# A graph network layer on one core: edge lists laid out ahead on the host, and the list test moved behind the first products

## The chip, the cores and the metric

The kernel runs on one core of one Trainium2 chip. The metric is the device time of one launch in microseconds; lower is better. The program's own names are used throughout: PE is the matrix engine, DVE the vector engine, ACT the scalar (activation) engine, POOL the general one, SP the engine that issues most of the transfers (DMAs). Each engine executes its own instructions in their order and waits where data or buffers are missing.

## What is computed

A graph with 1250 nodes of 1024 features and 41,250 directed edges (source, destination, type 0 or 1), sorted by destination, passes through two layers, each with a residual:

```
h = relu(layernorm(x))
# layer 0: relational convolution
n = ln_weight * h * rsqrt(mean(h*h) + 1e-6)
out = n @ W_root + bias
for r in (0, 1):                       # edge types
    w = (edge_type == r)
    sums = segment_sum(n[src] @ W_rel[r] * w, dst)
    out += sums / max(segment_sum(w, dst), 1)
x = x + h + elu(out) @ wo
# layer 1: attention over the same edges
h = relu(layernorm(x)) @ W
e = exp(-leaky_relu((h @ a_l)[src] + (h @ a_r)[dst], 0.1))
x = x + elu(segment_sum(e * h[dst], src) / (segment_sum(e, src) + 1e-5))
```

W_root and each W_rel[r] are 1024x286, wo is 286x1024, W is 1024x1024.

## The kernel before

Nodes are cut into ten row tiles of 128 (the last has 98). The gather and the sum over edges are done with a count matrix: for each pair of nodes and each edge type, how many edges join them. With it the sums over edges become matrix products, and both layers use it.

**Building the counts.** The sorted edges are cut into 110 groups of 375, and each group into three chunks of 125. For one chunk, DVE compares an index row with one number per edge and so gets a matrix of zeros and ones ("key", L505, 125x320), PE multiplies it with the one-hot matrix of the low seven bits of the source ("lo", L480, one for two groups) and adds up the three chunks of a group in PSUM (L506). ACT then copies the 16 destination columns of that group to their place in the counts (L513); where they start is read from a list at run time (L511). An edge that belongs to the next group's first destination is carried over (L509). All this holds only if a group's destinations lie within 16 nodes and neighbouring groups fit together. Where some group doesn't, a general version of the whole kernel (general_arm) does the work.

**The start (gnn_kernel, L1135 to L1234).** The three edge lists are loaded with 110 groups on the partitions. DVE makes the first and last destination of each group, counts the groups that don't fit (L1188 to L1199), and makes from the lists the numbers that the keys need; PE turns them so that the edges of a chunk lie on the partitions (L1221, L1227). Then every engine loads the count of misfits and branches (L1233, L1234): zero leads to fast_arm, and only there do norms and products begin. The given inputs lead to fast_arm.

**First stage of fast_arm (L469 to L654).** The order on PE, DVE and ACT is the one in which the code is written; no scheduler changes it. For each row tile there are 16 product steps (L648: two halves of the joined weights times eight blocks of 128 features). Between the product steps the code puts chunks of the count (`some`), as many as keep step with the products: five ahead, and the rest spread evenly over 154 of the 160 steps (L650). At fixed steps it also puts the statistics (L528), the norm (L541) and the transposes (L559) of tiles further on, and the three parts in which the last tile's product is scaled and split into three bf16 terms (L583 to L600). The statistics of tile t + 2 stand at steps 6 and 9 of tile t. Five buffers hold keys, so DVE can be at most five keys ahead of PE. POOL adds h to x by a transfer that accumulates (L573).

**Loads.** SP issues x's tile 0, the weights of eight blocks (two transfers for each block, W_rel and W_root, L1151 and L1152), tile 1 after the fourth block, and then the other tiles. A semaphore is used again after eight transfers, so an issue may have to wait until an earlier transfer has landed; the issues behind it wait too.

**After that** come the means (L711) and the way back through wo (L753), the attention layer's products (L787, L858), and its weights and sums (L931 to L998). The change doesn't touch them.

Of the kernel before, what the change touches and what calls it, by code (L numbers as in the profile page):

```python
# [8 lines left out]
F32 = mybir.dt.float32  # L9
# [401 lines left out]
def fast_arm(tc, ctx, w_root, conv_bias, wo, w_gat, a_gat, out,  # L411
             ident, eps5, eps6, lnw, const, wt, wcat, bias, xs, cnt_raw,
             meta, keys, lows, hot_ck, ck, bases, iota_lo, iota_key, iota_ck):
# [56 lines left out]
    with ExitStack() as c1:  # L470
        hot = c1.enter_context(tc.tile_pool(name="hot", bufs=5))
        work = c1.enter_context(tc.tile_pool(name="work1", bufs=2))
# [17 lines left out]
        def chunks():  # L490

            for q in range(NG):
# [10 lines left out]
                for j in range(J):  # L503
# [6 lines left out]
                    if j == J - 1:  # L510
                        b = nc.values_load(bases[0:1, q:q + 1], engines=[mybir.EngineType.Activation],  # L511
                                           min_val=0, max_val=N - 1)
                        nc.scalar.activation(cnt_w[:, :, bass.ds(b, W)], a3, AF.Copy)  # L513
# [21 lines left out]
        def norm(t):  # L535
            n, mv, rstd = ROWS[t], mvs.pop(t), rstds.pop(t)
            nc.vector.reciprocal(rstd[:n], rstd[:n])
            nmr = small("nmr")
            nc.vector.scalar_tensor_tensor(nmr[:n], mv[:n, 0:1], -1.0, rstd[:n], op0=ALU.mult, op1=ALU.mult)
            hs_[t] = h = work.tile([128, D], F32, name="h")  # L540
            nc.scalar.activation(h[:n], xs[t][:n], AF.Relu, bias=nmr[:n], scale=rstd[:n])  # L541
# [19 lines left out]
        def scaled(t, g):  # L561

            n, (hT, pts) = ROWS[t], hTs[t]
            for i in range(4):
                k = 4 * g + i
                if g == 0:
# [34 lines left out]

        for i in range(2):
            statistics(0, i)
        low_hots(0)
        carry_hots(0, 10)
        norm(0)
        some(4)
# [3 lines left out]
        some(1)  # L611
        scaled(0, 1)
        done, ahead = 5, 5
        SK = 2 * KD
        for t in range(T):
            pys[t] = ps.tile([128, 2, 512], F32, name="mm")
            for i in range(SK):
                r, k = divmod(i, KD)
# [9 lines left out]
                if t == 0 and i in (1, 2):  # L628
                    statistics(1, i - 1)
                if t == 0 and i == 3:  # L630
                    norm(1)
                if t == 0 and i in (5, 7):
                    square(i // 6)
# [16 lines left out]
                want = min(NG * J, ahead + -(-(NG * J - ahead) * (t * SK + i + 1) // (T * SK - 6)))  # L650
# [426 lines left out]
def gnn_kernel(  # L1077
# [12 lines left out]
    a_gat: bass.AP,  # L1090
    out: bass.AP,
):
    nc = tc.nc
    D = x.shape[1]
    F = w_root.shape[1]
    HF = F // 2
    KD = D // 128
    assert x.shape[0] == N and NG * GE == src.shape[0] and HF * 2 == F
# [4 lines left out]
    ident = const.tile([128, 128], F32, name="ident")  # L1103
    make_identity(nc, ident)
    ones = const.tile([128, 1], F32, name="ones")
    nc.vector.memset(ones, 1.0)
# [3 lines left out]
    nc.vector.memset(eps6, 1e-6)  # L1110
    lnw = const.tile([128, KD], F32, name="lnw")

    nc.scalar.activation(lnw[:, 0:1], eps5, AF.Sqrt)
    bias = const.tile([128, F], F32, name="bias")

    meta = const.tile([128, 2376], F32, name="meta")
    parts, at = [], 0
    for size in (NG * J, NG * J // 2, NG * T, 3 * 128, T * W, T, NG, NG + 1):
# [6 lines left out]
    iota_key, iota_ck, ck = parts[4].bitcast(F16), parts[5].bitcast(F16), parts[6]  # L1125
    info = parts[7][0:1].bitcast(I32)

    xs = [big.tile([128, D], F32, name=f"x{t}", tag=f"x{t}") for t in range(T)]
    cnt_raw = big.tile([128, 2 * T * NPAD], F16, name="cnt")


    wt = [big.tile([128, D + 2], F32, name=f"w{k}") for k in range(KD)]
    wcat = [w[:, :3 * F].rearrange("p (r f) -> p r f", r=2) for w in wt]

    with ExitStack() as ec:  # L1135
        ep = ec.enter_context(tc.tile_pool(name="ep", bufs=1))
        eps = ec.enter_context(tc.tile_pool(name="eps", bufs=2, space=PSUM))
        eraw = ep.tile([NG, 3, GE], I32, name="eraw")
        for i, (a, eng) in enumerate(((dst, nc.sync), (src, nc.scalar), (etype, nc.gpsimd))):
            eng.dma_start(eraw[:, i, :], a.rearrange("(q e) -> q e", q=NG))  # L1140
        lnw_row = ep.tile([KD, 128], F32, name="lnw_row")
        nc.scalar.dma_start(lnw_row, ln_w.rearrange("(k p) -> k p", p=128))
        nc.scalar.dma_start(bias, _bcast_rows(conv_bias, 128, F))

        def load_x(t):
            nc.sync.dma_start(xs[t][:ROWS[t]], x[t * 128:t * 128 + ROWS[t], :])

        load_x(0)
        for k in range(KD):
            ks = slice(k * 128, (k + 1) * 128)  # L1150
            nc.sync.dma_start(wcat[k][:, :, :F], w_rel[:, ks, :].rearrange("r p f -> p r f"))  # L1151
            nc.sync.dma_start(wcat[k][:, :, F:], w_root[ks, :].rearrange("p (r f) -> p r f", r=2))  # L1152
            if k == 3:
                load_x(1)
        for t in range(2, T):
            load_x(t)

        nc.gpsimd.iota(iota_lo, pattern=[[1, 128], [0, 2 * J]], base=0, channel_multiplier=0,
                       allow_small_or_imprecise_dtypes=True)
        nc.gpsimd.iota(iota_key, pattern=[[1, 2 * T * W]], base=0, channel_multiplier=0,  # L1160
                       allow_small_or_imprecise_dtypes=True)
        nc.gpsimd.iota(iota_ck, pattern=[[1, 2 * T]], base=1, channel_multiplier=0,
                       allow_small_or_imprecise_dtypes=True)
        nc.gpsimd.memset(cnt_raw.rearrange("p (c n) -> p c n", n=NPAD)[:, :, N:], 0.0)


        end = ep.tile([NG, 1], F32, name="end")
        nc.vector.tensor_scalar(end, ident[:NG, NG - 1:NG], N - 4096.0, 4096.0, op0=ALU.mult, op1=ALU.add)

        dstf = ep.tile([NG, GE], F32, name="dstf")  # L1170
        nc.vector.tensor_copy(dstf, eraw[:, 0, :])
        first = ep.tile([NG, 1], F32, name="first")
        nc.vector.tensor_reduce(first, dstf, AX.X, ALU.min)
        below = ep.tile([NG, 1], F32, name="below")
        nc.vector.tensor_scalar_add(below, first, -4096.0)
        pn = eps.tile([128, 1], F32, name="pn", bufs=1)
        nc.tensor.matmul(pn[:NG], ident[:NG, 1:NG + 1], below, start=True, stop=True)
        last = ep.tile([NG, 1], F32, name="last")
        nc.vector.tensor_reduce(last, dstf, AX.X, ALU.max)
        last2 = ep.tile([NG, 1], F32, name="last2")  # L1180
        nc.vector.tensor_reduce(last2, dstf[:, :GE - PE_], AX.X, ALU.max)
        after = ep.tile([NG, 1], F32, name="after")
        nc.vector.tensor_tensor(after, pn[:NG], end, ALU.add)

        step = ep.tile([NG, 1], F32, name="step")
        nc.vector.tensor_tensor(step, after, first, ALU.subtract)
        odd = ep.tile([NG, 1], F32, name="odd")
        nc.vector.tensor_scalar(odd, last, first, float(W), op0=ALU.subtract, op1=ALU.is_ge)  # L1188
        nc.vector.scalar_tensor_tensor(odd, step, float(W), odd, op0=ALU.is_gt, op1=ALU.add)
# [79 lines left out]
```

## Time and profile before

| what | us |
|---|---|
| three timed runs | 636.57, 637.62 (median), 639.51 |
| the profiled execution | 635.77 |
| its span in the profile | 634.0 |
| PE busy in the span | 608.8 (96%) |
| DVE busy | 394.4 (62%) |
| ACT busy | 190.7 (30%) |
| POOL busy | 40.1 (6%) |
| first stage's products (L648), 320 instructions, PE busy | 145.3 |
| counts (L506), 330 instructions, PE busy | 74.4 |
| keys (L505), 330 instructions, DVE busy | 85.4 |

A product step is two PE instructions, since the float32 product takes two passes. In a line of the timeline the first number is the start in the span, the second the time covered; then come the engine, the line of the kernel, the operation, what is written and read, how many instructions are merged into it, and in brackets how long the engine stood idle before it and who released it. Instructions on one engine overlap at their ends, so the mean duration of one is more than the distance from one to the next.

In a line of the windows each engine has its busy time and, in brackets, the number of its instructions, in the order PE, PE's weight loads, DVE, ACT, POOL; then come the clock that PE was granted (1.00 is full), the busy share of the 16 DMA engines, and GB/s.

### The profile page before, as it was taken

Reading aid. Unit: us, or ns where it says so; the run is one execution under the profiler, and the core shown is the slowest. Engines: PE = TensorE matmul, PEld = TensorE weight load, DVE = VectorE, ACT = ScalarE, POOL = GpSimd, SP = SyncE. Lnnn points to the kernel's source line nnn. Section 1 sums busy time; section 2 is a strip of 40 time slices with the busy share of each in tenths; the row PEclk is TensorE's granted clock in tenths of the full one; section 3 lists DMA queues with packets and bytes.
Section 4 is the critical chain, followed back from the end, with each engine's and each line's share of the span. In section 5 each row is a group of like instructions: output and inputs, shape, how many; then the busy total and the mean of one; then the engine's idle time right before and its main releaser. Section 6 shows DMA issues by size and latency. Waiting matters only on the chain.

```text
span 634.0 us, 7896 instructions
## 1 busy us (share of the span) xinstructions
PE 608.8 (96%) x2816; PEld 416.1 (66%) x2816; DVE 394.4 (62%) x969; ACT 190.7 (30%) x354; POOL 40.1 (6%) x52
## 2 busy tenths in 40 slices
PE   2999999999999999999999999999999999999995
PEld 1566666666656756767656888888766666666653
DVE  6788898988772798556676231215445556666642
ACT  2555555555542023320301232222022112222210
POOL 3100000000000000000000000000010111111110
PEclk9999999999999999999999999999999999999999
DMA  7961111011108400000092000000000000000001
GB/s 228 261 198 35 33 35 34 2 34 34 26 1 304 126 1 0 2 1 1 1 169 39 2 1 1 1 0 1 0 1 33 34 33 34 34 34 33 34 35 31
DMA packets 26634, 30.19 MB, mean 48 GB/s; under 512 B 14209, under 2 KB 19068, under 8 KB 26584
## 3 DMA queue, kind: packets, MB, share of 16 engines
q1 hardware_dynamic: 24059, 21.39, 11.3%
q0 software_dynamic: 1488, 5.29, 4.5%
q10 hardware_dynamic: 1037, 2.90, 1.5%
q8 instruction: 24, 0.39, 0.3%
q14 instruction: 26, 0.21, 0.1%
HBM read 16.06 MB, written 5.12 MB: 33 GB/s over the span
## 4 chain that ended last, share of the span: by engine, by line
PE 87%; DVE 5%; DMA 4%; SPq 1%; issue 1%; ACT 0%; ACTq 0%; POOL 0%; DVEq 0%; POOLq 0%
PE mm L648 18%; PE mm L982 16%; PE mm L858 11%; PE p L982 8%; PE acc L506 7%; PE mm L711 7%; PE z L858 4%; PE mm L753 4%; PE mm L787 3%; PE p L994 3%; DMA w<-in_L_gnn_W_rel_dram 2%; DVE scr L699 2%; PE p L787 1%; PE tp L559 1%; DMA rest_w<-in_L_gnn_wo_weight_dram 1%; DMA x<-in_x_dram 1%
## 5 line engine op out<-in xcount | busy, mean ns | idle before, releaser
L648 PE MATMUL mm<-w,hT 128*128 128x429 f32 (+1 forms) x320 | 145.3, 538 | 0.0
L982 PE MATMUL mm<-h,z 128*128 128x342 f32 (+1 forms) x360 | 118.5, 450 | 0.0
L505 DVE TENSOR_SCALAR key<-meta 125x320 bf16<-125x320 f16 x330 | 85.4, 300 | 20.9 <-PE acc L506 10.5
L982 PEld LDWEIGHTS mm<-h,z 128*128 128x128 f32 (+1 forms) x360 | 68.4, 190 | 34.9
L506 PEld LDWEIGHTS <-lo 125*128 125x128 bf16 x330 | 40.8, 126 | 58.0 <-issue 38.3
L506 PE MATMUL acc<-key,lo 125*128 125x320 bf16 x330 | 74.4, 306 | 4.3 <-DVE key L505 4.3
L711 PE MATMUL mm<-y,cnt 128*128 128x286 bf16 (+3 forms) x600 | 75.2, 284 | 3.1 <-DVE x L755 2.9
L513 ACT ACTIVATE cnt<-acc 128x320 f32 x110 | 49.9, 454 | 80.2 <-PE acc L506 72.2
L711 PEld LDWEIGHTS <-cnt 128*128 128x128 f16 (+1 forms) x600 | 59.4, 99 | 17.5 <-issue 4.1
L982 PE MATMUL p<-h,z 128*128 128x341 f32 (+1 forms) x180 | 66.1, 449 | 0.0
L648 PEld LDWEIGHTS mm<-w,hT 128*128 128x128 f32 (+1 forms) x320 | 51.3, 191 | 3.3 <-issue 2.1
L982 PEld LDWEIGHTS p<-h,z 128*128 128x128 f32 (+1 forms) x180 | 33.7, 188 | 17.7
L858 PE MATMUL mm<-w,a 128*128 128x257 f32 (+3 forms) x192 | 44.8, 380 | 0.0
L858 PEld LDWEIGHTS mm<-w,a 128*128 128x128 f32 (+1 forms) x192 | 35.6, 187 | 6.0 <-ACT h L884 0.4
L753 PE MATMUL mm<-wo,meta 128*128 128x512 f32 (+1 forms) x80 | 37.6, 592 | 0.0
L951 POOL TENSOR_TENSOR w<-w,x 128x1024 f32<-128x1024 f32 x9 | 23.4, 2597 | 135.3 <-ACT w L947 120.7
L931 DVE SCALAR_TENSOR_TENSOR z<-z 128x1280 f32<-128x1280 f32 (+2 forms) x11 | 31.2, 2847 | 0.3
L972 DVE TENSOR_SCALAR inv<-mm 128x1 f32<-128x1 f32 x9 | 1.4, 158 | 47.6 <-PE mm L982 47.6
L934 ACT ACTIVATE z<-z 128x1280 f32<-128x1280 f32 (+2 forms) x11 | 12.9, 1173 | 58.8 <-DVE z L933 58.8
L480 DVE TENSOR_TENSOR lo<-meta 125x768 bf16<-125x768 f16 x55 | 30.2, 549 | 0.0
L947 ACT ACTIVATE w<-mm,inv 128x684 f32<-128x684 f32 x9 | 7.5, 832 | 74.2 <-DVE w L946 74.2
L935 DVE TENSOR_TENSOR z<-cnt,z 128x1280 f32<-128x1280 f16 (+2 forms) x11 | 15.1, 1371 | 13.4 <-ACT z L934 13.4
(181 smaller groups left out, 728.9 us busy)
## 6 DMA issues: line engine op xcount, KB each, us to landing
x<-in_x_dram SPq DMA_DIRECT2D x9, 512.0 KB, 5.0
x<-h POOLq DMA_DIRECT2D x9, 512.0 KB, 4.6
out_dram<-w SPq DMA_DIRECT2D x9, 512.0 KB, 3.0
w<-in_L_gnn_W_dram SPq DMA_DIRECT2D x8, 512.0 KB, 4.9
w<-in_L_gnn_W_rel_dram SPq DMA_DIRECT2D x8, 286.0 KB, 6.7
w<-in_L_gnn_W_root_dram SPq DMA_DIRECT2D x8, 143.0 KB, 4.5
wo<-in_L_gnn_wo_weight_dram ACTq DMA_DIRECT2D x2, 512.0 KB, 6.7
a<-in_L_gnn_a_dram ACTq DMA_DIRECT2D x2, 512.0 KB, 5.1
```

The lines of the kernel that those rows point to most:

```text
L480: nc.vector.tensor_tensor(los[q // 2], iota_lo, lows[:, q:q + 2, :].rearrange("p q j -> p (q j)")[:, None, :].to_broadcast([PE_, 128, 2 * J]),
L505: nc.vector.tensor_scalar(key, iota_key, keys[:, q, j:j + 1], None, op0=ALU.is_equal)
L506: nc.tensor.matmul(acc[:, :2 * T * W], los[q // 2][:, :, (q % 2) * J + j], key, start=(j == 0), stop=(j == J - 1))
L513: nc.scalar.activation(cnt_w[:, :, bass.ds(b, W)], a3, AF.Copy)
L648: nc.tensor.matmul(pys[t][:ROWS[t], r, :F + HF], hTs[t][0][:, k, :ROWS[t]], wcat[k][:, r, :], start=(k == 0), stop=(k == KD - 1))
L711: nc.tensor.matmul(pm[:n, r, :f], cnt[:k, h, r, t * 128:t * 128 + n], ybs[h][:k, s, r, :f], start=(h == 0 and s == 0), stop=(h == T - 1 an ...
L753: nc.tensor.matmul(po[:n, c, :], oT[:, i, :n], wo_of[i][:, cs], start=(i == 0), stop=False)
L787: nc.tensor.matmul(o, hT[:, k, :n], wg[k][:, c0:c1], start=(k == 0), stop=(k == KD - 1))
L858: nc.tensor.matmul(o[:a.shape[2], :c1 - c0], a[:, k, :], b[k][:, c0:c1], start=(start and k == 0), stop=(k == KH - 1), skip_group_check=no ...
L931: nc.vector.scalar_tensor_tensor(z, z, 0.1, z, op0=ALU.mult, op1=ALU.min)
L951: nc.gpsimd.tensor_add(high, high, xs[s][:n].rearrange("p (h c) -> p h c", h=2))
L982: nc.tensor.matmul(o, z[:ROWS[t], t, :n], hs[t][:ROWS[t], c0:c1], start=(t == 0), stop=(t == T - 1))
```

## The change

1. **Lists and weights laid out on the host.** Four more inputs are given, all of them rearrangements: the lists by edge within the chunk, group and chunk (`edges`, 125 rows of 990 numbers), every 375th destination (`firsts`), the first weights joined (`w_cat`, so that one transfer of 3432-byte rows loads a block), and ln_weight in columns. The transposes of the lists on PE go, with their copies out of PSUM.
2. **The loads first.** SP's loads of x and the weights are the first instructions of the kernel; lists, firsts and bias are loaded by ACT's queue, all three lists as one transfer.
3. **No branch at the start.** Norm, transposes and first products of tile 0 come ahead of the keys. The numbers for the keys are made on DVE between them. No key is made ahead; the count begins two steps late (`late = 2`). For tile 0 the product steps go block by block over both halves, statistics of tile 1 stand at steps 5 and 6 (1 and 2 before), its norm at step 7 (3 before), and the norm's h is written in two halves.
4. **The test later.** In step 1 of tile 1 DVE measures how far any edge lies outside of what the fast way allows, with a transpose on PE in the middle. In step 6 of tile 1 ACT branches on the result and would clear the counts; the other engines jump there too.
5. **The branch at the end.** fast_arm always runs; if the test found a misfit, general_arm runs after it and writes the output again.

The core of the diff:

```diff
-        for i in range(2):
-            statistics(0, i)
-        low_hots(0)
-        carry_hots(0, 10)
-        norm(0)
-        some(4)
+        room = [yh.tile([128, F + 3 * (F + 2)], F32, name=f"room{t}", tag=f"yh{t}") for t in (9, 8, 7)]
+        raw = room[0][:PE_, :3 * NG * J].bitcast(I32).rearrange("p (i q j) -> p i q j", i=3, j=J)
+        nc.scalar.dma_start(raw, edges)
+        nc.scalar.dma_start(first, _bcast_rows(firsts, PE_, NG))
+        nc.scalar.dma_start(bias, _bcast_rows(conv_bias, 128, F))
...
+        nc.gpsimd.tensor_copy(firstf, first)
+        nc.gpsimd.tensor_tensor(step[:, :NG - 1], firstf[:, 1:], firstf[:, :NG - 1], ALU.subtract)
...
+        nc.vector.tensor_scalar(tile_of, raw[:, 0], 7, None, op0=ALU.logical_shift_right)
+        norm(0)
+        nc.vector.scalar_tensor_tensor(block, tile_of, 2.0, raw[:, 1], op0=ALU.mult, op1=ALU.add)
+        nc.vector.tensor_tensor(d, raw[:, 2], first[:, :, None].to_broadcast([PE_, NG, J]), ALU.subtract)
+        nc.vector.scalar_tensor_tensor(keys, block, float(W), d, op0=ALU.mult, op1=ALU.add)
         for g in range(2):
             turn(0, g)
         scaled(0, 0)
-        some(1)
+        nc.vector.scalar_tensor_tensor(lows, tile_of, -128.0, raw[:, 0], op0=ALU.mult, op1=ALU.add)
         scaled(0, 1)
-        done, ahead = 5, 5
+        low_hots(0)
+        def carried():
+            nc.vector.tensor_tensor(ck, d[:, :, J - 1], step, ALU.is_equal)
+            nc.vector.scalar_tensor_tensor(ck, block[:, :, J - 1], 1.0, ck, op0=ALU.add, op1=ALU.mult)
+            carry_hots(0, 10)
+        def count_over():
+            nc.vector.tensor_tensor(over, d, limit, ALU.subtract)
+            nc.vector.scalar_tensor_tensor(over, d, -1.0, over, op0=ALU.mult, op1=ALU.max)
+            nc.vector.scalar_tensor_tensor(over[:, :, 0], step, -float(W), over[:, :, 0], op0=ALU.add, op1=ALU.max)
+            nc.vector.tensor_tensor(over[:, 0, 0:1], over[:, 0, 0:1], firstf[:, 0:1], ALU.max)
+            worst = small("worst")
+            nc.vector.memset(worst, 0.0)
+            nc.vector.tensor_reduce(worst[:PE_], over, AX.XY, ALU.max)
+            pt = bank("tp")
+            nc.tensor.transpose(pt[:1, 0, :], worst, ident)
+            nc.vector.tensor_reduce(worst[:1], pt[:1, 0, :], AX.X, ALU.max)
+            nc.vector.tensor_scalar_max(n_odd, worst[:1], 0.0)
+        def clear_if_odd():
+            odd = nc.values_load(n_odd, engines=[mybir.EngineType.Activation], min_val=0, max_val=8192)
+            with tc.If(odd > 0):
+                nc.scalar.activation(cnt_raw, eps6.to_broadcast([128, 2 * T * NPAD]), AF.Copy, scale=0.0)
+        done, ahead, late = 0, 0, 2
...
-                r, k = divmod(i, KD)
+                r, k = divmod(i, KD) if t else (i % 2, i // 2)
...
-                if t == 0 and i in (1, 2):
-                    statistics(1, i - 1)
                 if t == 0 and i == 3:
+                    carried()
+                if t == 0 and i in (5, 6):
+                    statistics(1, i - 5)
+                if t == 0 and i == 7:
                     norm(1)
...
+                if t == 1 and i == 1:
+                    count_over()
+                if t == 1 and i == 6:
+                    clear_if_odd()
...
-                want = min(NG * J, ahead + -(-(NG * J - ahead) * (t * SK + i + 1) // (T * SK - 6)))
+                want = min(NG * J, -(-NG * J * max(t * SK + i + 1 - late, 0) // (T * SK - 6 - late)))
...
+    load_x(0)
+    for k in range(KD):
+        nc.sync.dma_start(wt[k][:, :3 * F], w_cat[k * 128:(k + 1) * 128, :])
+        if k == 3:
+            load_x(1)
+    for t in range(2, T):
+        load_x(t)
...
-    n_odd = nc.values_load(info[0:1, NG:NG + 1], min_val=0, max_val=4 * NG + N)
-    with tc.If(n_odd == 0) as which:
-        with ExitStack() as arm:
-            fast_arm(...)
-    with which.Else():
+    with ExitStack() as arm:
+        fast_arm(...)
+    odd = nc.values_load(n_odd, min_val=0, max_val=8192)
+    with tc.If(odd > 0):
         with ExitStack() as arm:
             general_arm(...)
```

## The prediction

> **What bounds the kernel now.** I read the page first. TensorE (PE) is busy 96% of the span and holds 87% of the chain that ended last; of the 40 slices only the first is nearly empty. So time can be won only ahead of the first products and wherever PE waits later in that stage. Next I read the timeline from 0 to 40 us: which instruction opens each step, and what released it.
>
> ```profile
> 12.05 0.14 DVE L1199 TENSOR_TENSOR meta<-po,info_f 1x1 int32<-1x1 f32 x1 [0.68 <-PE po L1195]
> 12.95 1.29 DVE L528 BATCH_NORM_STATS2 st<-x 128x6 f32<-128x512 f32 x2 [0.75 <-DMA w<-in_L_gnn_W_root_dram]
> 15.49 1.24 ACT L541 ACTIVATE h<-x,nmr,rstd 128x1024 f32<-128x1024 f32 x1 [0.68 <-DVE nmr L539]
> 18.87 1.64 PE L648 MATMUL mm<-w,hT 128*128 128x429 f32 x2
> 26.92 0.69 DVE L528 BATCH_NORM_STATS2 st<-x 128x6 f32<-128x512 f32 x1 [1.51 <-DMA x<-in_x_dram]
> 28.70 0.91 PE L648 MATMUL mm<-w,hT 128*128 128x429 f32 x2
> ```
>
> The list test ends at 12.19; 0.76 us later, past the branch, the first statistics start; the first product starts at 18.87. Seen alone, that promises all the time from 5 to 19 us. But the fifth line shows a second gate: VectorE (DVE) waits 1.51 us for the third row tile (x2), and PE then stands until the next keys. The chain of waits over the first 36 us says it more strongly: up to 26.92 it runs through loads, not through the test.
>
> ```profile
> 1.64 6.75 DMA w<-in_L_gnn_W_rel_dram
> 9.21 3.14 DMA w<-in_L_gnn_W_rel_dram
> 12.96 4.43 DMA w<-in_L_gnn_W_rel_dram
> 20.91 5.99 DMA x<-in_x_dram
> 26.92 0.69 DVE st L528
> ```
>
> From 28.35 us PE runs with almost no gap to the stage's end at 197. Hence my yardstick is not the first product but the **eighth** of tile 0 (i = 7), the first one behind the wait for x2: 28.70 before. What is won there, less PE work that is put off and new stalls, is won at the end: the later stages have the same instructions in the same order.
>
> **When x2 lands after the change.** Up to x2 the queues carry the lists (0.495 MB), firsts and bias (0.20), three row tiles (1.57) and eight weight tiles (3.51): 5.78 MB. What the 16 engines can do is in the windows (the last two columns are DMA share and GB/s):
>
> ```profile
> 6.00:8.00 2.00, 0.61 (x3) 0.45 (x3) 2.00 (x8) 0.02 (x1) 0.07 (x1) 1.00 0.89 285
> 8.00:10.00 2.00, 0.72 (x4) 0.63 (x4) 1.79 (x7) 0.50 (x1) 0.00 (x0) 1.00 0.49 166
> 20.00:22.00 2.00, 1.78 (x7) 0.70 (x6) 2.00 (x7) 0.45 (x1) 0.00 (x0) 1.00 1.03 137
> 22.00:24.00 2.00, 2.00 (x10) 1.10 (x8) 1.93 (x8) 0.96 (x3) 0.00 (x0) 1.00 1.07 343
> 28.00:30.00 2.00, 1.65 (x10) 1.22 (x11) 1.97 (x9) 1.77 (x4) 0.00 (x0) 1.00 1.01 236
> ```
>
> The queue was already nearly full (share about 1), apart from holes such as 8 to 10 where SP waits for a semaphore. The change saves holes and small pieces (16 weight transfers become 8 with rows of 3432 bytes), not bytes. I take 343 GB/s: 5.78 MB = 16.9 us. To it come the start of data at 1.8 us (the window 0 to 2 moved only 50 KB), the residual transfer of tile 0, which falls inside this stretch (software queue: 4.5% of 634 us for ten = 2.85 us each), and 1.0 us until a waiter sees the last byte (between 0 and 1.6: DVE saw the destination list at 4.48, while it and the source list, 0.32 MB, need 1.1 us at 285 GB/s from 1.8). x2 lands at **22.5 us** instead of 26.9. Bounds: 419 GB/s, the best window (204 to 206 us), with the residual hidden gives 16.6; 236 GB/s gives 30.1.
>
> [...]
>
> **What stands before that gate.** x0 is now SP's first issue, at 0.74; the row tiles' shortest landing is 4.0 us and the median of the page 5.0, so about 5.3. From statistics to the start of h took 2.54 us (12.95 to 15.49); one list operation (shift, 0.84 on 375 elements; I take 0.5) is put between; half of h is 0.62, four transposes 1.06, one scaling 0.28, hand-overs 0.1: first product at 5.3 + 5.1 = 10.4 us, against 18.87. If the lists land after x0's statistics, that shift holds the reciprocal behind it on DVE, then ACT's h and PE; up to 10 us that costs nothing, since x2 is late anyway. Then PE does seven products (0.72 each in the chain) and nine key matmuls (0.135); DVE makes keys from about 12.5, does the carry flags, the statistics of tile 1 and stands at x2's statistics at about 17.7. So it is the load that ends last, by 4.8 us. The list work moved here (block, difference, keys, lows, carry: seven DVE operations of 0.23 to 0.55, about 3 us) lies in that wait and costs nothing; without it, some 2 us. The POOL operations (firsts, steps, limits) stand ahead of tile 0's residual or in its shadow; nobody waits before the test.
>
> **At the eighth product.** After x2: statistics 0.65, two keys 0.43, hand-over, two key matmuls: x2 + 1.3 = 23.8 us. Before it was 28.70. **Gained 4.9.**
>
> **What is given back.**
> 1. Norm of tile 1 now comes after x2's first statistics: its h (1.24) delays the first transposes, 1.98 us from the eighth to the ninth product against 1.52 before, of which half is made up by the key matmuls: **0.25**.
> 2. Keys put off: by the seventh product 18 were done before (5 ahead and 13), now 9 (two slots late). Nine times 0.135: **1.2** of PE time later. Nothing hides it, PE being the bound.
> 3. The test, now in tile 1 on a DVE that is busy 15.4 us in 18. Two operations of 330 elements (0.81 and 0.76 on 572: 0.47 + 0.44), one of 110 (0.33), single elements and a clear (0.23), a reduction (0.52) = 2.0; PE's transpose 0.34; reduction and clamp 0.41; the next key 0.25: **3.0** between one key and the next. PE holds the transpose in order, with product, keys and everything else behind it. Cover: five key tiles, about 2.4 slots of 1.05 us. DVE's own waits show how much it stays ahead:
>
> ```profile
> 38.09 0.52 DVE L505 TENSOR_SCALAR key<-meta 125x320 bf16<-125x320 f16 x2 [0.53 <-PE acc L506]
> 40.19 0.52 DVE L505 TENSOR_SCALAR key<-meta 125x320 bf16<-125x320 f16 x2 [0.48 <-PE acc L509]
> 43.59 0.30 DVE L505 TENSOR_SCALAR key<-meta 125x320 bf16<-125x320 f16 x1 [0.51 <-PE acc L506]
> 53.98 0.52 DVE L505 TENSOR_SCALAR key<-meta 125x320 bf16<-125x320 f16 x2 [0.42 <-PE acc L506]
> ```
>
> Where DVE waits for PE its lead is full. From 43.59 to 53.98 it never waits: that lead is used up. So only the waits between test and that stretch (0.48 + 0.51) absorb anything: 3.0 - 1.0 = **2.0**. Bounds 0.5 (the five tiles cover it) and 3.3 (nothing does).
> 4. Branches: every engine jumps once in tile 1, ACT also loads the register. The old test and branch took 0.76 us in all, and ACT is idle almost half this stage: **0.2**, bounds 0 and 0.8. The last branch lies beside the last store (issued until 629.20, span end 634.0): nothing; uncovered, 0.76.
>
> **Sum:** 4.9 - 0.25 - 1.2 - 2.0 - 0.2 = 1.25, say **1.3 us faster**. The profiled execution took 635.77 (span 634.0 and 1.77 around it) and would become 634.5; the three timed runs have a median of 637.62, and carried there it is **636.3 us**.
>
> **Rivals.**
> *The load comes early* (36%). At 370 GB/s, between 343 and the best window, and with the residual half hidden, x2 lands at 15.6 + 1.4 + 2.8 = 20; the key lead covers half the test. Eighth product at 21.3: 7.4 - 0.25 - 1.2 - 1.0 - 0.1 = 4.9 faster, 632.7. For it: large rows, fewer issues, and holes like 8 to 10 us that go. Against: 236 GB/s with row tiles alone at 28 to 30, at full share.
> *The load comes late, slower* (16%). In the new instruction order SP's fourth weight load waits for the lists' semaphore, then x1's load for x0's and the next ones for the first weights'; if the lists are late, the queue behind them runs dry and x2 lands at 26 (a mean of 285 GB/s, as at 6 to 8 us). Eighth product at 27.3: 1.4 - 0.25 - 1.2 - 3.3 - 0.5 = 3.9 slower, 641.5. With my test cost it decides from x2 landing at 23.75 on. For it: the holes of before are waits of the same kind; against: eight transfers may be outstanding.
> *The work is not really ahead* (within the forecast): the first product may start at 10.4 or 14 without changing the end, so an early first product alone proves no gain.
>
> **Chances.** The forecast has 48% (634.4 to 640.8), the early load 36%, the late one 16%. A measurement of this kernel tells about 0.5% (3.2 us) from no change, so faster 0.36, same 0.48, slower 0.16. Range 631.5 to 640.8: from the early case with the best cover and a run's scatter of 1 us to the edge of the late case.
>
> **What would show it.** Right: first product near 10 to 12 us, DVE waiting some 3 to 5 us for x2 at its statistics, PE idle beside it, eighth product near 23.8; a PE gap of up to 2 us at the transpose of the test, small gaps until the end of tile 1; from the means on, everything shifted by one amount. Wrong: no wait for x2 (the DMA term falls), a wait for the lists above 10 us, a gap at the branches over 1 us, or a longer tail behind the last store.

## The result, and the profile after

| | before | after |
|---|---|---|
| median of ten runs (lowest to highest), us | 637.47 (636.22 to 639.51) | 641.13 (640.48 to 643.32) |
| profiled execution; its span | 635.77; 634.0 | 640.75; 638.9 |
| x2 at its statistics | 26.92 | 25.73 |
| eighth product of tile 0 | 28.70 | 27.20 |
| end of the first stage (third part of the last tile) | 200.04 | 202.45 |
| split of wo's last rows (high_w) | 211.15 | 215.68 |
| last DVE operation | 627.74 | 632.24 |

After over before is 1.0061, 95% interval 1.0046 to 1.0076: **slower by 0.6%**, 3.7 us, where 1.3 us faster was forecast. The pair of profiles differs by more (5.0 us), since before's profiled execution is faster than any of its timed runs in the table; a second pair of profiles, below, differs by 5.3.

The timeline of after, in the same columns as in the prediction:

```profile
7.45 1.29 DVE L535 BATCH_NORM_STATS2 st<-x 128x6 f32<-128x512 f32 x2 [6.49 <-DMA x<-in_x_dram]
11.54 0.33 DVE L627 TENSOR_SCALAR room<-room 125x330 int32<-125x330 int32 x1 [2.55 <-DMA room<-in_edges_dram]
15.21 4.44 PE L706 MATMUL mm<-w,hT 128*128 128x429 f32 x6
25.73 0.69 DVE L535 BATCH_NORM_STATS2 st<-x 128x6 f32<-128x512 f32 x1 [3.05 <-DMA x<-in_x_dram]
26.68 0.42 PE L513 MATMUL acc<-key,lo 125*128 125x320 bf16 x1 [2.75 <-DVE key L512]
27.20 1.64 PE L706 MATMUL mm<-w,hT 128*128 128x429 f32 x2
40.97 0.27 PE L654 MATMUL tp<-ident,worst 128*1 128x128 f32 x1 [0.85 <-DVE worst L652]
```

The form is the forecast one: an early first product (15.21, before 18.87), then DVE standing for x2 and PE for the keys behind it. But the lists land only at 11.54 and x2 at 25.73, and the eighth product takes 1.64 us (0.91 before). The chain of waits now runs to x2 through the small `firsts`, which lie behind the lists:

```profile
1.39 12.44 DMA meta<-in_firsts_dram
13.85 0.33 SPq L1177
14.18 0.04 issue
14.22 0.48 SPq L1177
14.70 0.04 issue
14.75 10.96 DMA x<-in_x_dram
25.73 0.69 DVE st L535
```

Among the waits of SP's queue in the first 30 us, one stands out (total, times, longest):

```profile
SPq L1177 <- DMA room<-in_edges_dram: 8.7, 1, 8.7
```

And the windows (columns as before):

```profile
6.00:8.00 2.00, 0.00 (x0) 0.00 (x0) 0.55 (x1) 0.00 (x0) 0.00 (x0) 1.00 1.04 295
8.00:10.00 2.00, 0.00 (x0) 0.00 (x0) 0.95 (x3) 0.29 (x1) 0.00 (x0) 1.00 0.72 202
10.00:12.00 2.00, 0.00 (x0) 0.00 (x0) 0.43 (x3) 0.00 (x0) 0.00 (x0) 1.00 0.32 127
26.00:28.00 2.00, 1.32 (x5) 0.84 (x5) 1.97 (x9) 0.86 (x1) 0.00 (x0) 0.53 1.02 416
28.00:30.00 2.00, 2.00 (x11) 1.17 (x10) 1.97 (x8) 0.84 (x2) 0.92 (x1) 0.62 1.03 420
```

From 10 to 12 us the transfer engines are busy to 0.32: SP's fourth weight load waits for the lists' semaphore, and what still moves is mostly the rest of the loads that SP had issued ahead of it (0.19 of the 0.25 MB) and the lists. The old hole at 8 to 10 is shallower (0.72 instead of 0.49), and a deeper one has come. Before the keys PE stands for 2.75 us, and then its granted clock is 0.53 and 0.62 for four microseconds.

Followed step by step, after's lead over before is 1.50 us at the eighth product, 0.28 at the ninth, 0.26 at step 0 of tile 1; it is 0.90 behind at step 1 (the test's transpose), 1.14 behind at step 2, 2.41 at the stage's end. So the first stage accounts for half of the profiles' loss. Another 2.1 us lie between its end and high_w, the first operation on the tile rest_w, which holds wo's last rows. The chain of waits of after shows that stretch:

```profile
195.20 2.90 PE mm L706 x8
198.12 9.01 DMA w<-in_L_gnn_W_dram
207.14 8.42 DMA rest_w<-in_L_gnn_wo_weight_dram
215.68 0.69 DVE high_w L740
```

The same chain in a second profile of before (f1 below):

```profile
195.74 7.72 DMA w<-in_L_gnn_W_dram
203.46 0.02 issue
203.48 8.25 DMA rest_w<-in_L_gnn_wo_weight_dram
211.74 0.03 issue
```

ACT's fourth load of rest_w waits for the semaphore of the sixth tile of W (the attention layer's weights), whose load starts when the last products let go of the tile. It took 9.0 us in after. In before's own profile the chain does not run through W here: it comes past POOL's clear of rest_w, and the fourth load is issued at 203.36 without a wait. ACT's issues of the four loads, in before, in after and in g1 (below):

```profile
201.88 1.88 ACTq L680 DMA_DIRECT2D rest_w<-in_L_gnn_wo_weight_dram  x4
204.29 3.18 ACTq L738 DMA_DIRECT2D rest_w<-in_L_gnn_wo_weight_dram  x4
204.38 1.88 ACTq L741 DMA_DIRECT2D rest_w<-in_L_gnn_wo_weight_dram  x4
```

From high_w to the last DVE operation both first profiles take 416.6 us; the tail behind it grew from 6.26 to 6.66.

### The profile page after: what moved, and what is told of

Its sections match the earlier page's. It is cut to its first block, busy times and chain, and to the rows that moved or that the text cites. A ratio compares the mean times of both kernels' runs of the same rounds, so it can differ in the third digit from the quotient of the medians.

```text
span 638.9 us, 7847 instructions
## 1 busy us (share of the span) xinstructions
PE 607.6 (95%) x2804; PEld 414.8 (65%) x2804; DVE 392.3 (61%) x961; ACT 189.0 (30%) x351; POOL 42.9 (7%) x57
## 3 DMA queue, kind: packets, MB, share of 16 engines
q1 hardware_dynamic: 20738, 21.23, 10.9%
## 4 chain that ended last, share of the span: by engine, by line
PE 87%; DMA 6%; DVE 5%; issue 0%; SPq 0%; ACT 0%; ACTq 0%; DVEq 0%
PE mm L706 17%; PE mm L1040 16%; PE mm L916 11%; PE p L1040 8%; PE acc L513 7%; PE mm L769 7%; PE z L916 4%; PE mm L811 4%; PE mm L845 3%; PE p L1052 3%; DVE scr L757 2%; DMA meta<-in_firsts_dram 2%; DMA x<-in_x_dram 2%; PE p L845 1%; DMA w<-in_L_gnn_W_dram 1%; DMA rest_w<-in_L_gnn_wo_weight_dram 1%
## 5 line engine op out<-in xcount | busy, mean ns | idle before, releaser
L706 PE MATMUL mm<-w,hT 128*128 128x429 f32 (+1 forms) x320 | 147.0, 545 | 0.1
L568 PE MATMUL tp<-ident,h 128*128 128x128 f32 (+1 forms) x80 | 12.7, 287 | 13.1 <-ACT h L550 13.1
```

The lines of the kernel that those rows point to most:

```text
L706: nc.tensor.matmul(pys[t][:ROWS[t], r, :F + HF], hTs[t][0][:, k, :ROWS[t]], wcat[k][:, r, :], start=(k == 0), stop=(k == KD - 1))
```

## The experiments

Ratios are against the kernel before on the same chip, with 95% intervals; "stretch" is the time from the first stage's end to high_w.

**e1: the list tile with 128 rows.** Padded on the host by three rows that nobody uses; firsts are loaded to 128 rows too.

```diff
-        raw = room[0][:PE_, :3 * NG * J]...
-        nc.scalar.dma_start(first, _bcast_rows(firsts, PE_, NG))
+        raw = room[0][:, :3 * NG * J]...
+        nc.scalar.dma_start(first, _bcast_rows(firsts, 128, NG))
-    'edges': lists.reshape(3, NG, J, PE_).transpose(3, 0, 1, 2),
+    'edges': _np.pad(lists.reshape(...).transpose(3, 0, 1, 2), ((0, 3), (0, 0), (0, 0), (0, 0))),
```

> The changed kernel with the list tile and the firsts loaded as 128 rows (three rows of filler) instead of 125; nothing else. Theory A (the 125-row transfer runs on five engines: the windows at 10 to 12 us show a DMA share of 0.32; the lists land at 11.5, SP's fourth weight load waits for them, and x2 lands at 25.7): lists land at 5.5 to 7, no window under 0.8 before 20 us, x2 lands at 21.5 to 23, the eighth product starts near 23.5 instead of 27.2, and the time is 637.0 to 638.5 (3 us under the changed kernel's 641.1). Theory B (bytes bound the load anyway, the loss is in the test and the keys put off): lists early, but x2 not before 24.5, time 640 or more.

Measured: 638.15, ratio 1.0016 (0.9998 to 1.0035). DVE never waits for the lists, x0's statistics start at 5.96, the first product at 10.93. The first key behind x2, in PE's timeline, and the windows around it:

```profile
22.81 0.30 PE L515 MATMUL acc<-key,lo 125*128 125x320 bf16 x1 [4.07 <-DVE key L514]
```

The windows' columns are those of before:

```profile
20.00:22.00 2.00, 0.00 (x0) 0.00 (x0) 0.14 (x1) 0.00 (x0) 0.00 (x0) 1.00 1.03 422
22.00:24.00 2.00, 1.19 (x5) 0.66 (x5) 1.97 (x8) 0.72 (x1) 0.00 (x0) 0.90 1.02 420
24.00:26.00 2.00, 2.00 (x10) 1.55 (x9) 1.97 (x9) 0.98 (x2) 0.92 (x1) 0.50 1.01 412
26.00:28.00 2.00, 2.00 (x8) 0.99 (x7) 1.00 (x4) 0.45 (x2) 0.00 (x0) 0.75 1.04 408
```

x2 is at its statistics at 21.86, 3.9 us sooner for three rows, and the eighth product at 23.16: within 0.7 us of the prediction's 22.5 and 23.8. So its sum of bytes fits a load that uses all engines, and the 125 rows are what broke it. Yet the stage's end comes only 3.5 us sooner (198.92): PE now stands 4.07 us, and although the low clock lasts as long as in after (in the windows of either 1.7 us of clock are missing, 3.4 us at one half), more of it falls on work: ninth to tenth product take 1.61 us, in after 1.02.

**e2: without the test.** This leaves the test of the lists out (misfits are set to zero). Diff: the calls of count_over and clear_if_odd go.

> The changed kernel without the test of the lists and without the branch in tile 1 (the result is set to zero at the start, so misfits are not looked for); the branch at the end stays. Theory A (load): the gap of 0.85 us at the test's transpose goes, and some 1.2 us up to tile 1's second product; time 639.5 to 640.2. Theory B (the test and the branches on five engines are the main loss): 637.5 to 638.5. Prediction's own size for test and branches: 2.2 us, 638.9.

Measured: 639.71, ratio 1.0049 (1.0032 to 1.0065), stage's end 201.58: 0.8 to 0.9 us won. Step by step the test is worth more. At step 0 of tile 1 e2 is 0.50 behind after, since its low clock comes later (0.50 from 28 to 30 us, 0.73 from 30 to 32) and falls on the tenth product too; at step 2 it is 0.85 ahead. So the test's own place gives 1.35 us, and the clock takes 0.5 of it back.

**e3: tile 2's statistics later.**

```diff
-                    if i in (6, 9):
-                        statistics(t + 2, (i - 6) // 3)
-                    elif i == 11:
+                    if i in ((6, 9) if t else (11, 12)):
+                        statistics(t + 2, i // 9 if t else i - 11)
+                    elif i == (11 if t else 13):
                         norm(t + 2)
-                    elif i == 13:
+                    elif i == (13 if t else 14):
```

> The changed kernel with the statistics of tile 2 at steps 11 and 12 of tile 0 instead of 6 and 9 (norm at 13, square at 14); the loads as they are. If the wait for x2 on DVE, with PE idle behind it from 24.0 to 26.7 and at half clock until about 29, is what costs: no DVE wait for x2, granted clock 1.00 throughout, eighth product near 24.3, time 638 to 639. If PE stands for the weights instead (they land before x2 in the same queue) or DVE falls behind later: a wait for a weight tile at steps 8 to 12, time within 1 us of 641.1.

Measured: 640.03, ratio 1.0051 (1.0033 to 1.0069). The wait for x2 and the low clock are gone, the eighth product comes at 23.63, but by the ratio only 0.6 us are won (the first stage of the profile, one of the faster runs, ends 1.6 us sooner, at 200.88). PE then stands for keys in short pieces (0.54 and 0.39 us ahead of the ninth product, 1.25 ahead of the fifteenth) and 1.10 us at the test; ahead of the first two DVE had waited 1.82 us for ACT in tile 1's norm, ahead of the third 1.99 in tile 2's. Neither theory had that; the weights were not it.

**e4: before with joined weights only.** Diff: the two weight loads of a block become one of w_cat, in the kernel before.

> The kernel before with one part of the change alone: each block's first weights joined on the host and loaded by one transfer of 3432-byte rows (8 issues instead of 16). If x2's landing (26.9) is the gate of the kernel before, it lands at 23 to 24.5, the eighth product starts 2.5 to 3.5 us earlier and the time is 634 to 635.5 against 637.5. If the list test and the branch at 12.2 us are the gate, nothing changes: 637 to 638.

Measured: 637.41, ratio 1.0016 (1.0006 to 1.0025). DVE no longer waits for x2 (statistics at 25.33, eighth product 27.89, stage's end 199.72, 0.3 sooner), and nothing is won at the end: by the ratio it is 1.0 us slower, and its stretch is 12.1 (before 11.1). Large rows alone give 0.8 us at the gate.

**e5: e1 and e3 together.**

> The new kernel with both edits: lists and firsts loaded as 128 rows, and tile 2's statistics at product steps 11 and 12 of tile 0. Theory A (what the first stage loses behind the list load is PE standing for DVE, which stands for x2): with x2 landed near 21.9 as with 128 rows alone and nobody standing for it, the eighth product comes near 17 us, PE keeps its full clock, the first stage ends 1 to 2 us earlier than with 128 rows alone (198.9), and the time is 636 to 637. Theory B (the loads as a whole are the gate, x2 only the first to show it): PE then stands for the fifth to eighth weight tiles instead, the stage ends within 0.5 us of 198.9 and the time stays near 638.

Measured: 634.46, ratio 0.9965 (0.9951 to 0.9979); the eighth product at 18.39, no window under a clock of 1.00, stage's end 195.65. By the ratios the two edits give 6.1 us where each alone gave 2.9 and 0.6: with x2 early, the late statistics have something to uncover. The gain is larger than theory A's.

**e6: e1 without the test** (left out as in e2).

> Lists and firsts as 128 rows, and without the list test (that part of the computation is left out; the misfit count is set to zero). Theory A (the test costs about 0.9 us of PE time wherever the loads stand, as it did when it alone was left out): 637.2, stage end 198.0. Theory B (the prediction's price of the test, 2.2 with its branch, was hidden when the test alone was left out, because the stage had slack from the late x2): 636, stage end 196.7.

Measured: 635.63, ratio 0.9981 (0.9967 to 0.9995), stage's end 196.99. Taken out here, the test gives 1.9 us of stage and about 2.2 of time, near the prediction's 2.2 and theory B's figures. But theory B's reason, a price hidden by the late x2, is not what the steps show: e6 leads e1 by 0.58 at the tenth product already (26.87 against 27.45, its low clock comes earlier: 0.54 from 22 to 24 us), and by 1.92 at step 2 of tile 1. The test's own place gives 1.34, as in e2. Of the 0.58, 0.20 stand at the eighth product (x2 was there sooner), and the rest is where the low clock falls.

**e7, e8: wo's last rows loaded by POOL**, in the new and the old kernel.

```diff
-        nc.scalar.dma_start(rest_w[32 * i:32 * i + FR], wo[256:F, :])
+        nc.gpsimd.dma_start(rest_w[32 * i:32 * i + FR], wo[256:F, :])
```

> The new kernel with the four loads of wo's last rows issued by POOL, behind its clear of the same tile, instead of by ACT behind the loads of wo. Theory A (a good part of the loss lies behind the first stage, where ACT's fourth load of these rows waits for a late tile of the second weights): the 13.2 us from the stage's end to the split of these rows shrink to 10 or 11 and the time falls by 1.5 to 2.5, to 638.6 to 639.6. Theory B (that wait is hidden by PE's own work there, or the data come no sooner): within 0.7 us of 641.

> The kernel before with the same edit: the four loads of wo's last rows issued by POOL. Theory A (the wait for the second weights lengthens this stretch in the new kernel only, by about 1 to 2 us): the time falls by less than 0.7, and the distance between new and old kernel, both with the edit, comes to 2 to 2.8 us, the difference of their first stages and tails. Theory B (both kernels have that wait, and the shorter stretch in the profile of before was chance): both fall alike by 1.5 to 2.5 and the distance stays near 3.7.

Measured: 644.87 (1.0129, 1.0112 to 1.0146) and 641.65 (1.0077, 1.0059 to 1.0094), both worse, with stretches of 12.45 and 12.33. The edit also moved high_w behind other work on DVE, so it says little on the wait. The time is lost behind high_w, 421.2 and 421.3 us to the last DVE operation instead of 416.6; the distance of the two, 3.2 us, lies between the theories.

**e9: the lists on POOL's software queue**, still 125 rows, so that SP doesn't wait for them. Diff: `nc.scalar.dma_start(raw, edges)` becomes `nc.gpsimd.dma_start(raw, edges)`.

> The new kernel with the list tile (still 125 rows) issued by POOL's software queue, behind its iotas, so that no load of SP's waits on the lists' semaphore any more. Theory A (five engines carry the list, and as every later load is spread over all engines, its last part lies behind the list there, whether SP is held or not): x2 still lands at 25 to 26 us and the time stays within 0.7 us of the new kernel's 641. Theory B (SP's fourth weight load, held until the lists have landed, is what makes x2 late): with SP free, the queues stay full, x2 lands by 23.5 and the time falls to 638 to 639.5, though the lists themselves come later.

Measured: 640.34, ratio 1.0054 (1.0036 to 1.0071). Of DVE's timeline, the first list operation and x2's statistics:

```profile
14.54 0.33 DVE L627 TENSOR_SCALAR room<-room 125x330 int32<-125x330 int32 x1 [5.42 <-DMA room<-in_edges_dram]
25.67 0.70 DVE L535 BATCH_NORM_STATS2 st<-x 128x6 f32<-128x512 f32 x1 [1.13 <-DMA x<-in_x_dram]
```

x2 lands no sooner, as theory A said, though no hole is left from 10 us on (shares of 0.97 to 1.06). But the windows show another price: before the lists have landed, all queues together move 235 GB/s (10 to 12 us) and 302 (12 to 14), against 394, 402 and 417 in the three windows from 14 to 20. So it stays open whether the 125 rows would also have cost 3 us without holding SP.

**e10: PE kept busy while it waits.** Sixteen unread transposes behind the seventh product.

```diff
+                if t == 0 and i == 6:
+                    pt = bank("tp")
+                    for _ in range(16):
+                        nc.tensor.transpose(pt[:, 0, :], ident, ident)
```

> The new kernel with 16 transposes of the identity that nobody reads (about 0.15 us each, 2.4 us) on PE behind the seventh product, where PE stands for 2.7 us for the keys behind x2. Theory A (the lowered clock after that idle time costs 1 to 1.5 us): the granted clock stays at 1.00 from 26 to 30 us, the eighth to eleventh products close up, and the time falls by 0.8 to 1.3 against the new kernel, to 639.8 to 640.3. Theory B (the slow products only use time that the keys would not fill anyway, or the clock drops all the same): within 0.4 us of 641.

The two windows in which after's clock was low:

```profile
26.00:28.00 2.00, 1.07 (x6) 0.66 (x5) 1.97 (x8) 0.61 (x1) 0.00 (x0) 1.00 1.03 420
28.00:30.00 2.00, 1.99 (x12) 1.21 (x11) 1.97 (x9) 0.97 (x2) 0.92 (x1) 1.00 1.03 422
```

Measured: 639.30, ratio 1.0050 (1.0033 to 1.0067). The clock holds, eighth to ninth product take 1.91 us instead of 2.74, the stage's end comes 0.77 sooner: the low clock cost **0.8 us**. Unlooked for, the stretch fell from 13.2 to 11.2.

The profile of e7, whose first stage is after's, has the same without a transpose:

```profile
27.10 0.30 PE L513 MATMUL acc<-key,lo 125*128 125x320 bf16 x1 [3.41 <-DVE key L512]
26.00:28.00 2.00, 0.90 (x5) 0.65 (x5) 1.82 (x7) 0.44 (x1) 0.00 (x0) 1.00 1.04 424
28.00:30.00 2.00, 1.99 (x11) 1.12 (x10) 1.97 (x8) 1.14 (x2) 0.89 (x1) 1.00 1.04 424
```

PE stood 3.41 us, longer than in after, and the clock stayed at 1.00; eighth to ninth product take 1.91 us there too. So the price stands twice, but it is not shown that the transposes are what held the clock.

**e11, f4: without the last branch** and the general version (not entered by these inputs), in the new kernel and in e12.

> The new kernel without the last load of the misfit count, the last branch and the general version behind it (which the given inputs don't enter). Theory A (the tail of the profile has grown by 0.4 us, from 6.26 to 6.66): 640.7. Theory B (the general version, now behind the fast one in the program, costs more outside of what the span shows): 639 to 640. The prediction had put it at nothing: 641.1.

> The fastest form (lists as 128 rows, late statistics, spread test) without the last load of the misfit count, the last branch and the general version. Theory A (the profile's tail of 6.8 us shrinks to 4.4 and so does the time): 629.2. Theory B (what leaves the tail comes back elsewhere, as when it was left out of the new kernel): 631.6 within 0.5.

Measured: 641.19 (1.0070, 1.0054 to 1.0087) and 630.30 (0.9886, 0.9868 to 0.9905). The profile's tail falls by 2.4 to 2.6 us in both, from 6.66 to 4.23 and from 6.83 to 4.19. By the ratios f4 wins 2.0 us and e11 nothing; in e11's profile the first stage ends 1.0 us later than in after's, the stretch is 1.0 longer (14.2) and another 0.9 are lost behind high_w, which together takes the tail's gain back. Of the stage's 1.0, 0.3 stand at the eighth product (27.52), and the rest is the low clock, which comes later than in after and falls on more work; eighth to tenth product take 4.41 us, in after 3.76:

```profile
28.00:30.00 2.00, 1.99 (x11) 1.41 (x10) 1.97 (x8) 1.21 (x2) 0.82 (x1) 0.67 1.03 418
30.00:32.00 2.00, 2.00 (x7) 0.83 (x6) 1.21 (x5) 0.10 (x1) 0.09 (x1) 0.50 1.03 404
```

The longer stretch and the 0.9 stay open. The kernels of e12 and f4 have no low clock at that place, so f4's 2.0 says more about the tail. Before has a branch and a tail of that kind too, so the change's part is the 0.4 between 6.26 and 6.66.

**e12: lists as 128 rows, late statistics, and the test spread** as single operations over tiles 2 and 3, its transpose three places (six product steps) behind the reduction. The whole computation.

```diff
-                if t == 1 and i == 1:
-                    count_over()
-                if t == 1 and i == 6:
+                if t in (2, 3) and i % 2 == 0:
+                    next(count, None)
+                if t == 4 and i == 6:
                     clear_if_odd()
```

> Whole computation. Lists and firsts as 128 rows, tile 2's statistics at steps 11 and 12 of tile 0 (its norm at 14, the squares of tiles 1 and 2 at 13 and 15), and the list test cut into single operations spread over tiles 2 and 3, with the transpose two steps behind the reduction, so that PE never stands for it. Theory A (what the first two leave is the test, 2.2 us of standing and delayed keys, and the wait of tile 2's norm for ACT): first stage ends at 193.5 to 194.5 instead of 195.65, time 632 to 633.5. Theory B (DVE is the bound in the first tiles, and its test operations cost the same wherever they stand): within 0.7 us of 634.5.

Measured: 631.58, ratio 0.9918 (0.9901 to 0.9934), stage's end 193.01: better than theory A and than both kernels, 5.1 us under before. PE doesn't stand at the test any more:

```profile
62.60 0.27 PE L662 MATMUL tp<-ident,worst 128*1 128x128 f32 x1
```

**f1, f3: second profiles of before and after; f2: before with the four added inputs handed over, unused.**

> The kernel before, unchanged, a second profile. Theory A (the short stretch of 11.1 us from the first stage's end to the split of wo's last rows was chance): it takes 12 to 13 us here, with ACT's four loads of these rows issued over 2.4 us or more. Theory B (it belongs to the kernel): 11.0 to 11.4 again, issued over 1.9.

> The new kernel, unchanged, a second profile. If its stretch belongs to it, 12.5 to 13.5 us again; if it is chance of the transfers, anything from 11 to 14. First stage's end within 0.7 us of 202.45, x2 landed within 0.5 us of 25.7, the clock down to 0.5 to 0.65 in the windows from 26 to 30 us.

> The kernel before with the four added inputs declared and handed over, but used by nobody. Theory A (where the tensors lie in memory decides how fast the second weights come): the stretch grows to 12.4 to 13.3 us and the time by about 1 to 1.5 us, ratio 1.002. Theory B (it doesn't matter): ratio 1.000 within its interval, stretch as in the other look at before.

Measured: 636.61 and 641.89 (one run each); f2 637.39, ratio 1.0012 (1.0003 to 1.0022). Stretches: 11.80, 13.15, 10.92. So before and f2 have 10.9 to 11.8 and after has 13.2 twice: the longer stretch goes with the new kernel and not with where the tensors lie. (f2's 0.8 us by the ratio come from elsewhere: its first stage ends at 201.25, since DVE stands 1.84 us for ACT in tile 0; why is open.) What goes with the longer stretch is one packet. In two-microsecond parts of after (from 200.5) and of f1 (from 191.5), the queues hold (packets, MB, share of the engines; then issues, KB, us to landing), first in after:

```profile
q1 hardware_dynamic: 388, 0.75, 100.7%
q8 instruction: 1, 0.02, 3.1%
issues: line engine op xcount, KB each, median us to landing
w<-in_L_gnn_W_dram SPq DMA_DIRECT2D x1, 512.0 KB, 15.1
```

and in f1:

```profile
q1 hardware_dynamic: 33, 0.07, 25.2%
q8 instruction: 1, 0.02, 3.4%
issues: line engine op xcount, KB each, median us to landing
w<-in_L_gnn_W_dram SPq DMA_DIRECT2D x2, 512.0 KB, 4.9
```

A 16 KB fetch of instructions that takes one engine 1 us (3.1 and 3.4% of sixteen engines' two microseconds) falls ahead of W's tiles in before and among them in after, where the last tile takes 15.1 us to land. Over the 18 profiles up to here: where the fetch starts 3.9 to 8.0 us ahead of the stage's end (the five of the old form, and e10) the last data packet of W is through 5.6 to 7.7 us after that end; where it starts between 1.0 us ahead and 0.1 behind (the twelve others) 10.1 to 13.9. Being among W's packets is not enough: in e4 the fetch starts 3.1 us behind the first of them, and the last is through at 7.4.

In the traces of before and after each of the 24 packets on queue 8 has 16,384 bytes and takes 0.9 to 1.5 us. What goes with the fetch here is a delay of the data transfers beside it.

**g1, g2: the fetch moved.** The sixteen unread transposes of e10, but as PE's first instructions, ahead of tile 0's own, where PE is idle; in after and in e12.

> The new kernel with 16 transposes of the identity that nobody reads as PE's first instructions, where PE stands idle until tile 0's h (they are done by 10 us, so neither the clock at 26 to 30 us nor the order of the rest changes). Theory A (the place of the 16 KB instruction fetch among PE's instructions decides how late the second weights land): the fetch moves from 1.2 us before the first stage's end to about 8 us before, the last packet of the second weights comes 5 to 7 us after the end instead of 12, the stretch to the split of wo's last rows shrinks from 13.2 to 11 to 12 us with the first stage as it was (202.5), and the time falls by 1.0 to 2.0, to a ratio of 1.003 to 1.0045 against before. Theory B (the fetch only goes along with something else): stretch 12.5 to 14, ratio 1.006.

> The fastest whole computation (lists as 128 rows, late statistics, spread test) with the same 16 unread transposes first on PE. Theory A: fetch about 9 us before the first stage's end, stretch 11 to 12 instead of 13.0, time 629.8 to 630.6, ratio 0.989 to 0.990. Theory B: ratio 0.992, stretch 13.

The chain of g1 behind its last products:

```profile
198.20 7.63 DMA w<-in_L_gnn_W_dram
205.84 0.02 issue
205.86 8.69 DMA rest_w<-in_L_gnn_wo_weight_dram
214.54 0.03 issue
```

Measured: 639.37, ratio 1.0049 (1.0029 to 1.0069), and 630.63, 0.9908 (0.9896 to 0.9921). The fetch moved to 8.0 and 7.9 us ahead, the last packet of W came 7.3 and 6.7 us after the stage's end, ACT's four issues take 1.88 us again, the stretches fell to 12.1 and 11.1 with the first stages' ends as they were (202.53 and 193.18). So the place of the fetch is a cause of the longer stretch, worth 1.1 to 1.9 us there; in the times it shows as 0.6 to 0.8, less than expected, with overlapping intervals.

## Why the prediction was wrong, point by point

- **What bounds the kernel, and the yardstick: right.** The first product came 3.7 us sooner and decided nothing; the eighth behind x2 did.
- **When x2 lands: the step that failed.** 22.5 was forecast, 25.73 measured. The sum of bytes at 343 GB/s supposed that all engines work; e1, with 128 rows, lands at 21.86. The 125-row list tile left a share of 0.32 and held SP by its semaphore. The sign that it named for being wrong, a wait for the lists above 10 us, is there (11.54). The gain at the eighth product became 1.50 instead of 4.9.
- What the 125 rows cost: 3.2 us against the sum, 3.9 against e1. In after's trace never more than 6 of the lists' 125 packets (one row of 3,960 bytes each) are under way at once, from 1.66 to 10.88 us; of the bias's 128 packets on the same queue there are up to 13.
- **Norm of tile 1, 0.25: right in size** (0.39 is left of the 1.22 between eighth and ninth product once the clock is taken out).
- **The clock: missing.** 0.83 us here, and 0.8 to 1.5 in the seven profiles that have the low clock at this place, by how much of it falls on work. The prediction wanted PE idle beside a wait of 3 to 5 us and gave the work behind it no other speed.
- **Keys put off, 1.2: right.** From step 2 of tile 1 to the stage's end 1.27 us more are lost, as the nine keys are made up.
- **The test, 2.0: too large here.** 1.40 at its place (0.26 ahead to 1.14 behind); the same place gives 1.35 in e2 and 1.34 in e6. The 0.9 and 1.9 us by which their stages end sooner differ by what lies ahead of the test, the low clock above all.
- **The branches: none seen.** Between step 5 and step 7 of tile 1 the distance stays at 1.1.
- Added up: 1.50 - 0.39 - 0.83 - 1.40 - 1.27 = -2.39, against -2.41 at the stage's end.
- **"The later stages have the same instructions in the same order": true and not enough.** With another number of PE instructions ahead, the 16 KB fetch fell among the loads of W: 1.4 to 2.1 us in the two pairs of profiles (part of it shown by g1).
- **The tail at nothing:** 0.4 in the profiles.
- **The rival that came true** is the late load: 641.5 forecast, 641.1 measured, by the hold it named. But its test was dearer (3.3) and it had neither clock nor fetch, so its time was right in part by chance. The forecast's own last bound, 30.1 for x2, held the measured landing; the prediction gave this case 16% and ended its range at the edge of it.

The profiles' loss of 5.0 us is then 2.4 in the stage, 2.1 behind it and 0.4 in the tail. The medians' 3.7 is smaller, and no run divides it as finely.

## What to carry to other kernels

Choose the rows of a transfer before counting its bytes: here three rows of padding moved a landing by 3.9 us. A wait that stays in an engine's order takes back what an earlier start gives, so move the waiting instruction with the load (e5), and put a test in single operations where its reader is far behind (e12). Where every instruction of a later stage is unchanged, a shift in the instruction count can still cost that stage a microsecond (g1). And before two runs are compared for the price of one part, take out what the clock did in each: the test looked like 0.9 us in one pair and 1.9 in another, and was 1.35 in both.

## What the runs showed of the hardware that was not expected

- PE's granted clock fell to one half after waits of 2.75 us (after), 2.50 (e6) and 4.07 (e1), each time for 3.4 us by the windows, and stayed at 1.00 after one of 3.41 (e7). So the length of the wait alone does not decide; what does is not shown. What it costs depends on how much of the 3.4 us falls on work.
- From 12 to 18 us the windows show a clock of 1.00 for after and 0.50 for g1, yet in both kernels the second product starts 1.59 us behind the first and the third 1.43 behind the second, while the fifth to seventh follow at 1.02 to 1.08. So in after the 1.00 can't be what PE was granted there. Nothing rests on it, since x2 gates that stretch (eighth product 27.20 and 27.26).
- Before the lists had landed by the software queue, all queues together moved 235 and 302 GB/s, and 394 to 417 behind it (e9); whether the queue or the 125 rows slow them is not separated.
- One 16 KB instruction fetch, 1 us on one transfer engine (0.98 in after), goes with a last packet of 4 MB that comes 2 to 8 us later. Why it costs several times its own length stays open.
